# RWKV layers: the units' values repeated by DMA instead of by TensorE, the recurrence in place in SBUF

## The chip, the cores and the metric

The kernel runs on one core of one Trainium2 chip. The metric is the device time of one execution in microseconds. Each engine of the core has its own instruction queue: PE (TensorE, matmuls), DVE (VectorE), ACT (ScalarE), POOL (GpSimd) and SP (SyncE, which here only issues DMAs). ACT issues DMAs too. [...]

## The reference, cut to what matters

Four layers act on x (16 sequences, 100 steps, 512 channels): cross-attention, an RWKV block, cross-attention with a feed-forward part, and an RWKV block again. All is float32. The change is in the RWKV block alone, which runs as layer 1 and layer 3:

```python
w = exp(-exp(time_decay + tanh(xw @ td_w1) @ td_w2))     # b, l, 32 heads, 16
r, k, v = xr @ Wr.T, xk @ Wk.T, xv @ Wv.T                # the same shape
g = silu(xg @ Wg.T)
s = state[:, 2:18].reshape(b, 32, 16, 16)
for t in range(l):                                       # per head, i is the row, j the column
    a = k[t][i] * v[t][j]
    out[t][j] = sum_i r[t][i] * (u[i] * a + s[i, j])
    s = a + w[t][i] * s
x1 = x + (groupnorm(out) * g) @ Wo.T                     # then a channel mix with Wfk, Wfr, Wfv
```

Every state element s[i, j] is a first-order recurrence over 100 steps: it is multiplied by w[i] and k[i] * v[j] is added.

## The kernel before, in words

**Tiling.** The 16 sequences are taken in 4 groups of G = 4; a group has T = 400 columns (4 sequences of 100 steps). The 512 channels are 4 chunks of 128 (8 heads of 16). A pair of group and chunk is numbered C (16 per layer). A chunk has 8 x 16 x 16 = 2048 state elements, so its recurrence is cut in 8 units of 128 partitions x 2 rows x 400 columns. `where(u)` (L1129) gives chunk, column group jg (4 columns) and row pair rp of unit u; a layer has 128 units.

**One unit.** `spread(u)` (L1132) repeats the values v of 4 columns of each head over the partitions with two matmuls against the 0/1 matrix `sel`, shifted by one step, into a PSUM tile of two banks (`vbs`, two in turn); ACT copies the initial state `s0r` into the first step of each sequence. `product(u)` (L1147) multiplies this PSUM tile in place by the k of the row, an SBUF tile, on DVE. `scan(u)` (L1156) runs two tensor_tensor_scan on DVE, from the SBUF tile w and the PSUM tile into an SBUF tile `a`; POOL then multiplies `a` by r in place. `gather(p)` (L1166) sums two units' products over rows with eight matmul instructions into the PSUM bank `acc`, and `norm` (L1178) does the group norm once per chunk.

**Repeated rows.** k, w and r are needed with each row repeated over the partitions. ACT's queue stores them, as they are computed, in DRAM tiles (`store`, L806); `enter(C)` (L1089) loads the plain chunk of v, k and r, and `repeat(C, rp)` (L1099) loads k, w and r of a row pair with four DMAs of 32 partitions each, on SP. v is stored and loaded plain only.

**Order.** A loop over u (L1229 to L1285) writes out the order by hand for PE, DVE, ACT and POOL: wrappers pin the program order (`InOrder`, L69, `mm`, L81). SP's DMAs are not pinned. Each round does spread(u+1), product(u), deferred reads of PSUM banks (`slots.begin`), scan(u), the loads of the next chunk at fixed values of u % 8, gather, and then fills PE with `pieces` for a fixed number of microseconds (`due`, L1276): projections of the next group, output projections of the last one, and, in the last group, the channel mixes. Other PSUM work takes turns in three banks (`slots`, L652); taking a bank forces its outstanding read first.

**Weights** of 1 MB go through a ring of five tiles (`wring`, L42). The channel mix's three are loaded together 35 units before the end (L1247).

Of the kernel before, what the change touches and what calls it, by code (L numbers as in the profile page):

```python
# [35 lines left out]
def xattn_sequence(ctx: ExitStack, tc: tile.TileContext, d: dict, out: bass.AP):  # L36
# [41 lines left out]

    vector, scalar, gpsimd = InOrder(nc.vector), InOrder(nc.scalar), InOrder(nc.gpsimd)

# [555 lines left out]
    def rwkv(n, ws, next_weights, last):  # L636
# [6 lines left out]
        with ExitStack() as es:  # L643
# [5 lines left out]
            psum = es.enter_context(tc.tile_pool(name=f"l{n}a_ps", bufs=1, space=PSUM))  # L649
            vbs = [psum.tile([128, 2, 512], F32, name=f"vb{i}") for i in range(2)]  # L650
            acc = psum.tile([128, 512], F32, name="acc")
            slots = Slots([psum.tile([128, 512], F32, name=f"mm{i}") for i in range(3)])  # L652
            vec = rwkv_vecs(one, n)
# [34 lines left out]

            fold = one.tile([128, 32], F32, name="fold")
            nc.vector.tensor_reduce(fold, ident.rearrange("p (r s) -> p s r", s=32), AX.X, ALU.add)  # L690
            sel = one.tile([128, 16, 32], F32, name="sel")
            for j in range(16):
                nc.vector.tensor_copy(
                    sel[:, j, :].rearrange("p (h i) -> p h i", i=16),
                    fold.rearrange("p (h j) -> p h j", j=16)[:, :, j : j + 1].to_broadcast([128, 2, 16]),
                )


            share = one.tile([128, 2], F32, name="share")
            nc.vector.tensor_reduce(share, heads8.rearrange("p (q h) -> p h q", h=2), AX.X, ALU.add)  # L700
            nc.vector.tensor_scalar(share, share, -1.0 / 16, None, ALU.mult)
            gat = one.tile([128, 4, 32], F32, name="gat")
            nc.gpsimd.memset(gat, 0.0)
            for jg in range(4):
                nc.vector.tensor_copy(
                    gat[:, jg, :].rearrange("p (h g q) -> p g q h", g=4, q=4)[:, jg],
                    heads8.rearrange("p (q h) -> p q h", h=2),
                )
# [6 lines left out]
            s0r = one.tile([128, 4, NC, 4, B], F32, name="s0r")  # L715
            for r in range(4):
                rs = slice(32 * r, 32 * r + 32)
                ps = slots.bank()
                for c in range(NC):
                    for jq in range(4):  # L720
                        mm(
                            out=ps[32 * jq : 32 * jq + 32, c * 64 : (c + 1) * 64], lhsT=ident[rs, rs],
                            rhs=s0[rs, c].rearrange("p b (g q) -> p q g b", q=4)[:, jq],
                            start=True, stop=True,
                        )
                scalar.copy(s0r[:, r].rearrange("p c g b -> p (c g b)"), ps[:, : NC * 64])
# [51 lines left out]
            def chain(us, slot, tag, before, ps, lhs, rhs, read):  # L778
# [18 lines left out]
                piece(us / 2, second, slot, tag)  # L797

            def projections(g, base):
                nm = f"{n}_{g}"  # L800
                to = put[g] = {
                    t: dram.tile([NC, 4, 32, T], F32, tag=t, name=f"d{t}_{nm}")
                    for t in ("k", "v", "r", "w", "g")
                }

                def store(t, c, tile):  # L806
                    nc.scalar.dma_start(out=to[t][c].rearrange("r p t -> (r p) t"), in_=tile)

# [162 lines left out]
            def channels(g, slot):  # L971
# [41 lines left out]
                def keys(co):  # L1013
                    def read(ps):
                        if co == 0:
                            st["kk"] = two.tile([128, NC, T], F32, tag="kk", bufs=1, name=f"kk_{nm}")
# [19 lines left out]
                def values(i):  # L1036
                    b = g * G + i

                    def read(ps):
                        def add():  # L1040
                            th = st[i]
                            vector.scalar_tensor_tensor(th, th, 1.0, ps[:L, :], ALU.add, ALU.mult)
                            vector.scalar_tensor_tensor(xb[b], th, 0.5, xb[b], ALU.mult, ALU.add)
                            if last:
                                nc.sync.dma_start(out=out[b], in_=xb[b])

# [42 lines left out]
            def enter(C):  # L1089
# [4 lines left out]
                for k, bufs in (("v", 2), ("k", 1), ("r", 1)):  # L1094
                    t[k] = two.tile([128, T], F32, tag=f"{k}c", bufs=bufs, name=f"{k}c_{n}_{C}")
                    nc.sync.dma_start(out=t[k], in_=put[g][k][c].rearrange("r p t -> (r p) t"))
                repeat(C, 0)

            def repeat(C, rp):  # L1099
                g, c = C // NC, C % NC  # L1100
                rep = chunks[C]["rep"][rp] = {}
                for t in ("k", "w", "r"):
                    rep[t] = two.tile([128, 2, T], F32, tag=f"{t}rep", bufs=3, name=f"{t}r_{n}_{C}_{rp}")
                    for jq in range(4):
                        nc.sync.dma_start(
                            out=rep[t][32 * jq : 32 * jq + 32],
                            in_=put[g][t][c, 2 * rp : 2 * rp + 2].rearrange("r p t -> p r t"),
                        )

# [21 lines left out]

            def spread(u):  # L1132

                C, jg, rp = where(u)
                p4 = vbs[u % 2][:, :, :T].rearrange("p r (b t) -> p r b t", t=L)
                for i in range(2):
                    rs = slice(64 * rp + 32 * i, 64 * rp + 32 * i + 32)
                    mm(
                        out=p4[:, i, :, 1:L], lhsT=sel[rs, 4 * jg : 4 * jg + 4, :].rearrange("p q m -> p (q m)"),
                        rhs=steps(chunks[C]["v"][rs, :])[:, :, 0 : L - 1], start=True, stop=True,  # L1140
                    )
                g = C // NC
                scalar.copy(
                    p4[:, :, :, 0], s0r[:, 2 * rp : 2 * rp + 2, C % NC, jg, g * G : (g + 1) * G]
                )

            def product(u):  # L1147
                C, jg, rp = where(u)
                p4 = vbs[u % 2][:, :, :T].rearrange("p r (b t) -> p r b t", t=L)
                vector.tensor_tensor(  # L1150
# [5 lines left out]
            def scan(u):  # L1156
                C, jg, rp = where(u)
                rep = chunks[C]["rep"][rp]
                a = products[u] = two.tile([128, 2, T], F32, tag="a", bufs=4, name=f"a_{n}_{u}")
                for i in range(2):  # L1160
                    vector.tensor_tensor_scan(
                        a[:, i, :], rep["w"][:, i, :], vbs[u % 2][:, i, :T], 0.0, ALU.mult, ALU.add
                    )
                gpsimd.tensor_tensor(a, a, rep["r"], ALU.mult)
# [38 lines left out]
            def gates(C):  # L1203
# [3 lines left out]
                chunks[C]["g"] = two.tile([128, T], F32, tag="gc", bufs=5, name=f"gc_{n}_{C}")  # L1207
                nc.sync.dma_start(out=chunks[C]["g"], in_=put[g]["g"][c].rearrange("r p t -> (r p) t"))

# [21 lines left out]
            while u < UNITS + 6 or pieces or slots.due:  # L1231
# [6 lines left out]
                elif u % 32 == 0 and u > 0:  # L1238
# [7 lines left out]
                    output(g - 1, u + 7)  # L1246
                if u == UNITS - 32 - 3:  # L1247
                    cm.update(load(n, "Wfk", "Wfr", "Wfv"))
# [396 lines left out]
    def load(layer, *names):  # L1645
        return {k: load_w(d[f"L{layer}_{k}"], f"l{layer}_{k}") for k in names}

    ws1 = {}
    layer0(lambda: ws1.update(load(1, "Wk", "Wv", "Wr")))
# [72 lines left out]
```

## Time and profile before

| | |
|---|---|
| median of 3 runs | 3527.54 us (3523.34 to 3530.71) |
| profiled execution, its own time | 3530.07 us |
| its span, first to last instruction | 3528.3 us |
| PE busy | 3217.1 us (91%) |
| DVE busy | 1770.8 us (50%) |
| ACT busy | 981.8 us (28%) |
| POOL busy | 1376.4 us (39%) |
| DMA | 216.60 MB, mean 61 GB/s |
| layer 1, first product of the recurrence to the last | about 859 to 1499 us |
| layer 3, the same | about 2785 to 3425 us |

Busy times overlap, since engines run side by side. Shares over the whole span mix four layers with different limits; the two RWKV layers have to be read in their own windows. Almost all pinned instructions carry the line of the wrapper (L77 for DVE, ACT and POOL, L82 for matmuls), so they are told apart by tile names: `vb` is the PSUM tile of a unit, `a` its SBUF tile, `kr`, `wr`, `rr` the repeated rows, `dk`, `dv`, `dr`, `dw`, `dg` the DRAM tiles, `vc`, `kc`, `rc`, `gc` the plain chunks.

### The profile page before, as it was taken

The page shows a single profiled execution, that of the slowest core. Times are in us where ns is not written, and L with a number is a line of the kernel's source. Part 1 is how long each engine was busy: PE and PEld are TensorE (multiplying, and loading weights), DVE is VectorE, ACT ScalarE, POOL GpSimd, SP SyncE. Part 2 cuts the span into 40 slices and gives each one's busy share as a digit, 9 for nine tenths or more (in the row PEclk, how much of TensorE's full clock was granted, in tenths as well). Part 3 has the DMA queues.
Part 4 walks back from the last instruction along what each step waited for, and adds up shares of the span by engine and source line. Part 5 has one row for each costly group of instructions (what it writes and reads, how often), then busy time and mean ns, then how long its engine had stood idle before and what let it go on. Part 6 is the DMA issues. An engine that isn't in the chain of part 4 may idle for free. (4 is left out here: it accounts for less than half of the span.)

```text
span 3528.3 us, 46276 instructions
## 1 busy us (share of the span) xinstructions
PE 3217.1 (91%) x17795; PEld 1432.9 (41%) x17795; DVE 1770.8 (50%) x3570; ACT 981.8 (28%) x1715; POOL 1376.4 (39%) x1036
## 2 busy tenths in 40 slices
PE   6899998868999988988999999789998899998898
PEld 3444443333333333334454555345553333333333
DVE  4777777723777665514333333310001477775651
ACT  1322223222233233321322223211112233333232
POOL 1444444443666665511212111210002466665551
PEclk8999999978999989999999999999997899998998
DMA  5000001012434441101000010110012243433310
GB/s 169 21 31 21 31 21 33 1 56 86 126 108 124 126 146 54 38 27 55 25 19 19 19 31 18 39 53 8 10 57 68 87 129 104 134 115 117 87 29 14
DMA packets 153426, 216.60 MB, mean 61 GB/s; under 512 B 23498, under 2 KB 132106, under 8 KB 153206
## 3 DMA queue, kind: packets, MB, share of 16 engines
q1 hardware_dynamic: 130166, 180.87, 17.3%
q10 hardware_dynamic: 23040, 32.78, 2.6%
q8 instruction: 140, 2.29, 0.3%
q14 instruction: 80, 0.66, 0.1%
HBM read 174.25 MB, written 36.04 MB: 60 GB/s over the span
## 5 line engine op out<-in xcount | busy, mean ns | idle before, releaser
L77 POOL TENSOR_TENSOR a<-a,rr 128x800 f32<-128x800 f32 x256 | 480.9, 1879 | 342.4 <-DVE a L77 269.7
L77 DVE TENSOR_TENSOR_SCAN a<-wr,vb 128x400 f32<-128x400 f32 x512 | 475.7, 971 | 19.8 <-PE acc L82 10.9
L77 DVE TENSOR_TENSOR vb<-vb,kr 128x792 f32<-128x792 f32 x256 | 250.5, 979 | 197.0 <-ACT vb L77 195.5
L77 DVE CUSTOM_DVE_ANT_0 junk<-l_sc,mask 100x361 f32<-100x361 f32 x512 | 273.0, 533 | 90.1 <-PE l_sc L82 73.6
L82 PE MATMUL vb<-vc,sel 32*128 32x396 f32 x1024 | 261.0, 568 | 3.4 <-DVE a L77 2.2
L77 DVE TENSOR_TENSOR pt<-l_sc,maskT 121x400 f32<-121x400 f32 x384 | 193.5, 566 | 89.9 <-PE l_sc L82 89.0
L77 ACT ACTIVATE pt<-pt 121x1600 f32<-121x1600 f32 x96 | 147.6, 1538 | 282.2 <-DVE pt L77 280.7
L1425 DVE CUSTOM_DVE_ANT_0 junk<-l2a_sc,mask 100x361 f32<-100x361 f32 x256 | 136.9, 535 | 172.9 <-PE l2a_sc L82 155.7
L77 POOL TENSOR_TENSOR xj<-tm,ext 128x400 f32<-128x400 f32 x160 | 152.8, 962 | 174.3 <-DVE tm L77 168.0
L77 DVE SCALAR_TENSOR_TENSOR tm<-mm,vec,sx 128x400 f32<-128x400 f32 x160 | 99.9, 631 | 235.6 <-PE mm L82 190.9
L1461 POOL TENSOR_TENSOR pa<-pt,pt 121x1600 f32<-121x1600 f32 x16 | 57.2, 3574 | 366.8 <-ACT pt L1456 366.8
L63 PE MATMUL h<-yTb,l_fc 128*128 128x400 f32 x512 | 175.3, 505 | 8.2 <-ACT yTb L229 8.2
L1642 DVE TENSOR_TENSOR x<-pb,x 100x512 f32<-100x512 f32 x16 | 12.8, 799 | 338.3 <-DMA pb<-po 332.7
L82 PE MATMUL v<-l_v_w,ct 128*121 128x512 f32 x384 | 180.0, 613 | 0.0
L82 PE MATMUL k<-ct,l_k_w 128*128 128x361 f32 x512 | 173.0, 481 | 7.3 <-DVE mv_l2a L207 7.3
L77 POOL TENSOR_TENSOR pa<-pt,pt 121x1600 f32<-121x1600 f32 x32 | 114.7, 3586 | 165.5 <-ACT pt L77 165.5
L63 PE MATMUL p<-l_proj,h 128*128 128x512 f32 x384 | 165.4, 592 | 0.0
L77 ACT COPY vb<-s0r 128x8 f32<-128x8 f32 x256 | 43.0, 168 | 408.7 <-PE vb L82 322.9
L82 PE MATMUL l_sc<-kz,qz 32*100 32x361 f32 x1024 | 117.1, 528 | 42.6 <-DVE pt L77 21.7
L82 PEld LDWEIGHTS vb<-vc,sel 32*128 32x128 f32 x1024 | 84.8, 190 | 146.9 <-issue 107.3
L82 PE MATMUL mm<-l_Wo,gc 128*100 128x512 f32 x256 | 124.6, 629 | 8.4 <-POOL gc L77 8.4
L63 PEld LDWEIGHTS h<-yTb,l_fc 128*128 128x128 f32 x512 | 98.1, 192 | 83.3 <-ACT yTb L229 10.1
(258 smaller groups left out, 5305.6 us busy)
## 6 DMA issues: line engine op xcount, KB each, us to landing
kr<-dk SPq DMA_DIRECT2D x256, 100.0 KB
wr<-dw SPq DMA_DIRECT2D x256, 100.0 KB
rr<-dr SPq DMA_DIRECT2D x256, 100.0 KB
ct<-in_ctxT SPq DMA_DIRECT2D x32, 722.0 KB
dk<-k ACTq DMA_DIRECT2D x32, 200.0 KB
kc<-dk SPq DMA_DIRECT2D x32, 200.0 KB
dw<-wd ACTq DMA_DIRECT2D x32, 200.0 KB
dv<-v ACTq DMA_DIRECT2D x32, 200.0 KB
```

What stands on the lines that cost most here:

```text
L63: nc.tensor.matmul(out=ps, lhsT=lhs(c), rhs=rhs(c), start=(c == 0), stop=(c == n - 1))
L77: return lambda *args, **kw: tc.keep_in_program_order(op(*args, **kw))
L82: pin(nc.tensor.matmul(**kw))
L1425: nc.vector.tensor_tensor_reduce(out=junk, in0=ss[r][:L, :S2], in1=t["mask"], scale=-1.0, scalar=FLT_MAX, op0=ALU.add, op1=ALU.min, accum_ ...
L1461: nc.gpsimd.tensor_tensor(t["pa"], t["pt"][0], pt, ALU.add)
L1642: nc.vector.tensor_tensor(x, pb[:, i, :], x, ALU.add)
```

## The change

The repetition of v leaves PE. v is stored in DRAM like k, w and r, one element later, so that a read which begins one element before a row is the row shifted by one step. `fetch(u)` reads it with two DMAs of 64 partitions straight into the SBUF tile `a` of the unit, which now has 6 buffers instead of 4, two rounds ahead. ACT's copy of the initial state (`first`) writes into `a` one round ahead. The product, the scans and POOL's multiplication all work in place in `a`.

The partitions of a unit are ordered head, row, column, where before they were ordered column, head, row; the DRAM layout of k, v, r, w puts the four row residues of a partition quartet next to each other, so a row pair is one run of 800 elements, and `repeat` needs one DMA of 128 partitions where it needed four. Stores and plain loads are now four DMAs of 32 partitions instead of one of 128. The loads of a chunk's repeated rows are spread over more rounds, and SP's DMAs in the loop are pinned in program order. The PSUM banks of `vbs` go to `slots`, which has 7 banks instead of 3. `gat` and the set-up of `s0r` follow the new order; `sel` is gone. The squared keys of the channel mix share a ring with its inputs. The channel mix's weights come in quarters, from 46, 40 and 35 units before the end.

```diff
-            vbs = [psum.tile([128, 2, 512], F32, name=f"vb{i}") for i in range(2)]
             acc = psum.tile([128, 512], F32, name="acc")
-            slots = Slots([psum.tile([128, 512], F32, name=f"mm{i}") for i in range(3)])
+            slots = Slots([psum.tile([128, 512], F32, name=f"mm{i}") for i in range(7)])
...
+            def rows_of(g, t, c):
+                if t == "g":
+                    return [(slice(0, 128), put[g][t][c].rearrange("r p t -> (r p) t"))]
+                rows = put[g][t][1:] if t == "v" else put[g][t]
+                rows = rows[c * 128 * T : (c + 1) * 128 * T].rearrange("(p r t) -> r p t", r=4, t=T)
+                return [(slice(32 * r, 32 * r + 32), rows[r]) for r in range(4)]
...
                 def store(t, c, tile):
-                    nc.scalar.dma_start(out=to[t][c].rearrange("r p t -> (r p) t"), in_=tile)
+                    for ps, rows in rows_of(g, t, c):
+                        nc.scalar.dma_start(out=rows, in_=tile[ps])
...
-            def repeat(C, rp):
+            def repeat(C, rp, names):
                 g, c = C // NC, C % NC
-                rep = chunks[C]["rep"][rp] = {}
-                for t in ("k", "w", "r"):
+                rep = chunks[C]["rep"].setdefault(rp, {})
+                for t in names:
                     rep[t] = two.tile([128, 2, T], F32, tag=f"{t}rep", bufs=3, name=f"{t}r_{n}_{C}_{rp}")
-                    for jq in range(4):
-                        nc.sync.dma_start(
-                            out=rep[t][32 * jq : 32 * jq + 32],
-                            in_=put[g][t][c, 2 * rp : 2 * rp + 2].rearrange("r p t -> p r t"),
-                        )
+                    x = put[g][t]
+                    n0 = x.offset + (c * 128 + 2 * rp) * T
+                    sync.dma_start(
+                        out=rep[t], in_=bass.AP(x.tensor, n0, [[4 * T, 32], [0, 4], [1, 2 * T]])
+                    )
...
-            def spread(u):
+            def fetch(u):
                 C, jg, rp = where(u)
-                p4 = vbs[u % 2][:, :, :T].rearrange("p r (b t) -> p r b t", t=L)
-                for i in range(2):
-                    rs = slice(64 * rp + 32 * i, 64 * rp + 32 * i + 32)
-                    mm(
-                        out=p4[:, i, :, 1:L], lhsT=sel[rs, 4 * jg : 4 * jg + 4, :].rearrange("p q m -> p (q m)"),
-                        rhs=steps(chunks[C]["v"][rs, :])[:, :, 0 : L - 1], start=True, stop=True,
-                    )
+                g, c = C // NC, C % NC
+                a = products[u] = two.tile([128, 2, T], F32, tag="a", bufs=6, name=f"a_{n}_{u}")
+                v = put[g]["v"]
+                for h in range(2):
+                    n0 = v.offset + (c * 128 + 64 * h + 16 * jg + 2 * rp) * T
+                    sync.dma_start(
+                        out=a[64 * h : 64 * h + 64],
+                        in_=bass.AP(v.tensor, n0, [[0, 16], [4 * T, 4], [1, 2 * T]]),
+                    )
+
+            def first(u):
+                C, jg, rp = where(u)
                 g = C // NC
                 scalar.copy(
-                    p4[:, :, :, 0], s0r[:, 2 * rp : 2 * rp + 2, C % NC, jg, g * G : (g + 1) * G]
+                    products[u].rearrange("p r (b t) -> p r b t", t=L)[:, :, :, 0],
+                    s0r[:, 2 * rp : 2 * rp + 2, C % NC, jg, g * G : (g + 1) * G],
                 )
...
             def product(u):
                 C, jg, rp = where(u)
-                p4 = vbs[u % 2][:, :, :T].rearrange("p r (b t) -> p r b t", t=L)
+                p4 = products[u].rearrange("p r (b t) -> p r b t", t=L)
                 vector.tensor_tensor(
                     p4[:, :, :, 1:L], p4[:, :, :, 1:L],
                     chunks[C]["rep"][rp]["k"].rearrange("p r (b t) -> p r b t", t=L)[:, :, :, 0 : L - 1],
...
-                a = products[u] = two.tile([128, 2, T], F32, tag="a", bufs=4, name=f"a_{n}_{u}")
+                a = products[u]
                 for i in range(2):
-                    vector.tensor_tensor_scan(
-                        a[:, i, :], rep["w"][:, i, :], vbs[u % 2][:, i, :T], 0.0, ALU.mult, ALU.add
-                    )
+                    vector.tensor_tensor_scan(a[:, i, :], rep["w"][:, i, :], a[:, i, :], 0.0, ALU.mult, ALU.add)
                 gpsimd.tensor_tensor(a, a, rep["r"], ALU.mult)
...
                 unit = 0 <= u < UNITS
+                if 0 <= u + 2 < UNITS:
+                    fetch(u + 2)
                 if 0 <= u + 1 < UNITS:
-                    spread(u + 1)
+                    first(u + 1)
                 if unit:
                     product(u)
...
                     if at == 4:
                         enter(C)
+                    elif at == 5:
+                        repeat(C, 0, "w")
                     elif at == 6:
-                        repeat(C, 1)
+                        repeat(C, 0, "r")
                         bonus(C, 0)
                     elif at == 7:
+                        repeat(C, 1, "kw")
                         bonus(C, 1)
                 C = u // 8
+                if 0 <= C < NC * NG and at == 0:
+                    repeat(C, 1, "r")
```

More of the change, by code (lines that the diff above doesn't have):

```diff
@@ L77, in __getattr__ @@
             return lambda *args, **kw: tc.keep_in_program_order(op(*args, **kw))
-    vector, scalar, gpsimd = InOrder(nc.vector), InOrder(nc.scalar), InOrder(nc.gpsimd)
+    vector, scalar, gpsimd, sync = map(InOrder, (nc.vector, nc.scalar, nc.gpsimd, nc.sync))
     def mm(**kw):
@@ L687, in rwkv @@
             nc.vector.tensor_tensor(center, ident, mean, ALU.subtract)
[L689 to L695, printed above, removed]
-                )
+            hq = one.tile([128, 2, 4], F32, name="hq")
+            nc.vector.tensor_reduce(hq, ident.rearrange("p (h i q) -> p h q i", h=2, q=4), AX.X, ALU.add)
             share = one.tile([128, 2], F32, name="share")
-            nc.vector.tensor_reduce(share, heads8.rearrange("p (q h) -> p h q", h=2), AX.X, ALU.add)
+            nc.vector.tensor_reduce(share, hq, AX.X, ALU.add)
             nc.vector.tensor_scalar(share, share, -1.0 / 16, None, ALU.mult)
@@ L705, in rwkv @@
                 nc.vector.tensor_copy(
-                    gat[:, jg, :].rearrange("p (h g q) -> p g q h", g=4, q=4)[:, jg],
-                    heads8.rearrange("p (q h) -> p q h", h=2),
+                    gat[:, jg, :].rearrange("p (h g q) -> p g h q", g=4, q=4)[:, jg], hq
                 )
@@ L715, in rwkv @@
             s0r = one.tile([128, 4, NC, 4, B], F32, name="s0r")
+            pair = one.tile([128, 32], F32, name="pair")
+            nc.vector.tensor_reduce(pair, ident.rearrange("p (r s) -> p s r", s=32), AX.X, ALU.add)
+            fold = two.tile([128, 4, 128], F32, tag="stage", bufs=6, name="fold")
+            nc.gpsimd.memset(fold, 0.0)
+            for q in range(4):
+                nc.vector.tensor_copy(fold[:, q, :].rearrange("p (s q) -> p q s", q=4)[:, q], pair)
             for r in range(4):
@@ L719, in rwkv @@
                 for c in range(NC):
-                    for jq in range(4):
+                    for q in range(4):
                         mm(
-                            out=ps[32 * jq : 32 * jq + 32, c * 64 : (c + 1) * 64], lhsT=ident[rs, rs],
-                            rhs=s0[rs, c].rearrange("p b (g q) -> p q g b", q=4)[:, jq],
-                            start=True, stop=True,
+                            out=ps[:, c * 64 : (c + 1) * 64], lhsT=fold[rs, q, :],
+                            rhs=s0[rs, c].rearrange("p b (g q) -> p q g b", q=4)[:, q],
+                            start=(q == 0), stop=(q == 3),
                         )
@@ L801, in projections @@
                 to = put[g] = {
-                    t: dram.tile([NC, 4, 32, T], F32, tag=t, name=f"d{t}_{nm}")
-                    for t in ("k", "v", "r", "w", "g")
-                }
+                    t: dram.tile([NC * 128 * T + (t == "v")], F32, tag=t, name=f"d{t}_{nm}") for t in "kvrw"
+                }
+                to["g"] = dram.tile([NC, 4, 32, T], F32, tag="g", name=f"dg_{nm}")
+                sync.dma_start(out=to["v"][0:1].rearrange("(p t) -> p t", t=1), in_=eps[0:1, :])
                 def store(t, c, tile):
-                    nc.scalar.dma_start(out=to[t][c].rearrange("r p t -> (r p) t"), in_=tile)
+                    for ps, rows in rows_of(g, t, c):
+                        nc.scalar.dma_start(out=rows, in_=tile[ps])
                 rows = [xb[g * G + i] for i in range(G)]
@@ L1015, in read @@
                         if co == 0:
-                            st["kk"] = two.tile([128, NC, T], F32, tag="kk", bufs=1, name=f"kk_{nm}")
+                            st["kk"] = two.tile([128, NC, T], F32, tag="xm", bufs=3, name=f"kk_{nm}")
                         rl = two.tile([128, T], F32, tag="tm", bufs=4, name=f"rl_{nm}_{co}")
@@ L1044, in add @@
                             if last:
-                                nc.sync.dma_start(out=out[b], in_=xb[b])
+                                sync.dma_start(out=out[b], in_=xb[b])
                         slots.read_later(ps, add)
@@ L1095, in enter @@
                     t[k] = two.tile([128, T], F32, tag=f"{k}c", bufs=bufs, name=f"{k}c_{n}_{C}")
-                    nc.sync.dma_start(out=t[k], in_=put[g][k][c].rearrange("r p t -> (r p) t"))
-                repeat(C, 0)
-            def repeat(C, rp):
+                    for ps, rows in rows_of(g, k, c):
+                        sync.dma_start(out=t[k][ps], in_=rows)
+                repeat(C, 0, "k")
+            def repeat(C, rp, names):
                 g, c = C // NC, C % NC
-                rep = chunks[C]["rep"][rp] = {}
-                for t in ("k", "w", "r"):
+                rep = chunks[C]["rep"].setdefault(rp, {})
+                for t in names:
                     rep[t] = two.tile([128, 2, T], F32, tag=f"{t}rep", bufs=3, name=f"{t}r_{n}_{C}_{rp}")
-                    for jq in range(4):
-                        nc.sync.dma_start(
-                            out=rep[t][32 * jq : 32 * jq + 32],
-                            in_=put[g][t][c, 2 * rp : 2 * rp + 2].rearrange("r p t -> p r t"),
-                        )
+                    x = put[g][t]
[3 more added lines that the diff above has]
+                    )
             def bonus(C, part):
@@ L1207, in gates @@
                 chunks[C]["g"] = two.tile([128, T], F32, tag="gc", bufs=5, name=f"gc_{n}_{C}")
-                nc.sync.dma_start(out=chunks[C]["g"], in_=put[g]["g"][c].rearrange("r p t -> (r p) t"))
+                sync.dma_start(out=chunks[C]["g"], in_=rows_of(g, "g", c)[0][1])
             def output(g, slot):
@@ L1246, in rwkv @@
                     output(g - 1, u + 7)
-                if u == UNITS - 32 - 3:
-                    cm.update(load(n, "Wfk", "Wfr", "Wfv"))
+                for k, at_u in (("Wfk", UNITS - 46), ("Wfr", UNITS - 40), ("Wfv", UNITS - 35)):
+                    if 0 <= u - at_u < NC:
+                        load_part(cm, n, k, u - at_u)
                 if u >= UNITS and not nws and not any(p[3] == ("wo", NG - 1) for p in pieces):
@@ L1646, in load, with load_part @@
         return {k: load_w(d[f"L{layer}_{k}"], f"l{layer}_{k}") for k in names}
+    def load_part(ws, layer, k, c):
+        if c == 0:
+            ws[k] = wring.tile([128, NC, 512], F32, tag="w", name=f"l{layer}_{k}")
+        sync.dma_start(out=ws[k][:, c, :], in_=d[f"L{layer}_{k}"][c * 128 : (c + 1) * 128, :])
     ws1 = {}
```

## The prediction

> **What bounds the kernel now.** I read the windows first, over the stretch of layer 1 in which groups 0 to 2 run their recurrence (860 to 1295 us) and its last group (1295 to 1486.5), then the same two of layer 3. The columns after the window's length are the busy us of PE, weight load, DVE, ACT and POOL, then the granted PE clock, the DMA share and GB/s.
>
> ```profile
> 860.00:1295.00 435.00, 417.80 (x1586) 158.08 (x1584) 319.96 (x396) 137.85 (x292) 288.45 (x231) 0.94 0.40 119
> 1295.00:1486.50 191.50, 169.98 (x573) 62.53 (x574) 109.60 (x136) 70.27 (x133) 106.66 (x93) 0.88 0.22 62
> 2775.00:3215.00 440.00, 421.87 (x1599) 161.39 (x1600) 316.96 (x392) 143.49 (x300) 290.90 (x238) 0.93 0.39 118
> 3215.00:3420.00 205.00, 180.45 (x613) 66.84 (x613) 116.97 (x146) 75.50 (x145) 112.59 (x96) 0.89 0.23 64
> ```
>
> PE is busy 418 of 435 us, DVE 320, POOL 288: PE is the bound, and DVE plus POOL together (608) exceed the window, so these two overlap today. The same windows restricted to the tile vb show 285 DVE instructions, three per unit (one product, two scans), so 95 units in the first stretch and, from 283, 94 in that of layer 3: 435/95 = 4.58 and 440/94 = 4.67 us per unit. The costliest groups give the pieces of a unit:
>
> ```profile
> L77 POOL TENSOR_TENSOR a<-a,rr 128x800 f32<-128x800 f32 x256 | 480.9, 1879 | 342.4 <-DVE a L77 269.7
> L77 DVE TENSOR_TENSOR_SCAN a<-wr,vb 128x400 f32<-128x400 f32 x512 | 475.7, 971 | 19.8 <-PE acc L82 10.9
> L77 DVE TENSOR_TENSOR vb<-vb,kr 128x792 f32<-128x792 f32 x256 | 250.5, 979 | 197.0 <-ACT vb L77 195.5
> L82 PE MATMUL vb<-vc,sel 32*128 32x396 f32 x1024 | 261.0, 568 | 3.4 <-DVE a L77 2.2
> ```
>
> The product and scans read one operand from PSUM (vb) and one from SBUF (kr, wr). After the change both operands are in SBUF. So I looked for DVE instructions that already have two SBUF operands. In the answer for tile x (min/median/max ns):
>
> ```profile
> L77 DVE TENSOR_TENSOR x<-mm,x x32: 691/692/694, 1044.0 to 3465.5; 100x512 f32<-100x512 f32 x32
> L77 DVE SCALAR_TENSOR_TENSOR x<-th_1b,x x16: 691/692/1650, 1341.4 to 1598.0; 100x512 f32<-100x512 f32 x16
> L1642 DVE TENSOR_TENSOR x<-pb,x x16: 691/693/1751, 2369.1 to 2668.5; 100x512 f32<-100x512 f32 x16
> ```
>
> With PSUM and SBUF (mm, x) none of 32 exceeds 694 ns; with two SBUF operands some take 1650 or 1751. The timeline around the 1650, DVE first and then POOL (start us, us):
>
> ```profile
> 1471.01 1.65 DVE L77 SCALAR_TENSOR_TENSOR x<-th_1b,x 100x512 f32<-100x512 f32 x1
> ```
> ```profile
> 1470.23 1.88 POOL L77 TENSOR_TENSOR a<-a,rr 128x800 f32<-128x800 f32 x1
> 1472.07 2.12 POOL L77 TENSOR_TENSOR sx_1b<-ext_1b 128x400 f32<-128x400 f32 x2
> ```
>
> POOL's product ends at 1472.11; the DVE instruction ends at 1472.66, 0.55 us later, where 0.69 is its own length. It stood still until POOL was done. The POOL pair then takes 2.12, not 2 x 0.854 = 1.71. Each side blocks the other, and a hand-over saves about 0.14 us (0.69 - 0.55).
>
> [...] The trace has 979 with a PSUM operand, and 692 against 693 at 512 elements for PSUM and SBUF, so I take no gain from leaving PSUM. [...]
>
> **The change part by part.**
> Removed: the spread matmuls. The tile's windows give PE 96.45 us in the first stretch, but some run beside matmuls of mm in other row groups (at 1074.12 both start together). Taking the union of PE's intervals without them leaves 354 of 418 us and 357 of 422 in the two long stretches, 144.5 of 170 and 152.6 of 180 in the last groups. So 64, 65, 25 and 28 us of PE work go. In the long stretches PE alone would allow (435 - 64)/95 = 3.9 us per unit.
>
> Moved to SBUF: per unit one product of 0.98 and two scans of 0.97, 2.92 us on DVE[...]. POOL's work reads SBUF, too, apart from 12 memsets of 0.1: 288.45/95 = 3.04 us per unit (the product 1.88, xj 0.60, the rest og, gc, rk, xm, sx). No two-SBUF scan is in the trace; bounds are that it holds the path for its 0.97 or not at all. I take the first, as it reads two SBUF streams like the product. Then DVE and POOL exclude each other: 2.92 + 3.04 = 5.96 us per unit. POOL has 209 instructions of size over 95 units, 2.2 per unit; each can be one hand-over to it and one back, so up to 4.4 x 0.14 = 0.62 is saved: 5.34 at best. Neither side runs while a result crosses (the scan pair that ends at 1087.66 releases the POOL product at 1087.88: 0.2 us), where the other has nothing ready. I take 5.34 + 0.16 = 5.5. DVE's other work, 51 us or 0.53 per unit, has a PSUM operand or one input; it can lie under POOL's time.
> Long stretches: 95 x (5.5 - 4.58) = +87, 94 x (5.5 - 4.67) = +78, together **+165 us**.
> Last groups: two-operand DVE 84.2 plus POOL 106.7 is 191, less 78 POOL instructions x 2 x 0.14 = 22: 169 to 191, in a window of 191.5; PE would need 144.5 plus its present idle 21.5. Between -22 and 0 each if only one bounds; the two chains wait on each other there, so I take 0.
>
> Added: the fetch, two transfers of 200 KB per unit, 95 x 0.41 = 39 MB on 52 MB now (119 GB/s x 435 us). Today's rate at full share is 119/0.40 = 297 GB/s, so 91 MB need 306 of 522 us. Hidden. One pair takes 0.41 MB/297 = 1.4 us[...]. It starts when gather has freed the product of unit u-4, in iteration u-1, and is wanted by the ACT copy in iteration u+1: at least one period, 5.5 us, covers it. That copy is a new wait: ACT's stores, tanh, exp and bank reads queue behind it, and PE waits for these. On SP, now in program order, the fetch stands behind chunk loads that wait for stores of k, v, r; issues cost 0.42 us each, some 35 per chunk against 28, 15 us of a chunk's 44: hidden. Taken at 0; if the cover goes, see the second rival.
> ACT: 12 more stores per chunk at 0.33 us, 4 us of 44 on an engine that is a third busy: 0. Seven banks in place of three: PE idles only 17 us in the stretch, and PE is no longer the bound: 0, at best -17 per layer. The sixteen set-up copies (173 ns each, 3 us) lie under the wait for the layer's loads: 0. Weight loads in quarters: 0.
>
> **Sum:** profiled execution 3530.07 (span 3528.3 and 1.8 around it) + 165 = 3695; the median shown, 3527.54, is 2.5 lower, so **3693**.
>
> **Rivals.**
> First, it is faster. [...] DVE's hold is 0.98 per unit; 0.98 + 3.04 = 4.0, or 3.7 with hand-overs, and PE bounds at 3.9: -65 and -65, and half of the last groups' 53: -26. That is -156, 3372; with some blocking of products, about 3400. The point of decision is a hold of 4.62 + 0.62 - 3.04 = 2.2 us per unit. For it: no two-SBUF scan is in the trace. Against it: all lengthened instructions are of the two-operand kind.
> Second, still slower. The fetch lands late: sixteen reads of the same rows at once, or SP held up. From 5.5 us after its gather on, ACT's copy stops DVE. At 1 us per unit it adds 189: 3880. For it: no such repeated read is in the trace. Against it: the DMA share of 0.58.
> Third, a small loss or none: hand-overs all saved (5.34: 72 + 63 = +135), last groups -44, banks worth -17 per layer: +57, 3584, or lower.
>
> **How the numbers follow.** The lock with the fetch hidden 0.70, with 3600 to 3850 as its own range (5.34 and -44 below; 5.96 + 0.2 per unit, 150 + 140 = +290 and 30 of new waits above); late fetch 0.10; faster 0.16; small loss or none 0.04. The range 3540 to 3880 holds the first, half of the second and the last, 0.79. A difference of 0.2% (7 us) is about what can be told: faster 0.16, same 0.03, slower 0.81.
>
> **What would show it.** Product and scan means rising from 0.98 and 0.97 towards 1.5 or more, and POOL's a from 1.88 to over 2.2, both by blocking; PE falling to about 75% in the long stretches; a unit of 5.5 us; DMA waits still small. I am wrong if scans keep 0.97 beside a running POOL product, or if the copy of the first state waits for DMA.

## The result and the profile after

The changed kernel takes 3736.14 us (3732.84 to 3737.62, 4 runs) against 3526.94 us, a ratio of 1.0592 (95% interval 1.0573 to 1.061). The profiled execution took 3736.31, its span is 3734.3. The forecast was 3693, range 3540 to 3880, so the loss is 209 us where 165 was forecast.

The costliest groups on DVE and POOL (busy us, mean ns, then the idle time in front and its releaser):

```profile
L77 DVE TENSOR_TENSOR_SCAN a<-wr,a 128x400 f32<-128x400 f32 x512 | 801.2, 1604 | 40.4 <-ACT a L77 33.8
L77 POOL TENSOR_TENSOR a<-a,rr 128x800 f32<-128x800 f32 x256 | 593.2, 2318 | 301.3 <-DVE a L77 97.4
L77 DVE TENSOR_TENSOR a<-a,kr 128x792 f32<-128x792 f32 x256 | 306.2, 1196 | 4.4 <-DMA a<-dv 4.4
L77 POOL TENSOR_TENSOR xj<-tm,ext 128x400 f32<-128x400 f32 x160 | 228.4, 1435 | 138.0 <-DVE tm L77 137.9
```

The last of them before the change:

```profile
L77 POOL TENSOR_TENSOR xj<-tm,ext 128x400 f32<-128x400 f32 x160 | 152.8, 962 | 174.3 <-DVE tm L77 168.0 <-DMA kr<-dk 4.7 <-DMA rr<-dr 1.1
```

The same instructions on the same shapes: the scan went from 971 to 1604 ns, the product from 979 to 1196, POOL's product from 1879 to 2318, its xj from 962 to 1435. Little idle time is left in front of the DVE instructions (4 us before the product, which had 197, and 40 before the scans, which had 20), so DVE looks like a busy engine. The distribution in the answer for tile a (min/median/max ns) shows that a good part of this is standing, which counts as busy: the scan's median is 1680 ns, its shortest 957.

```profile
L77 DVE TENSOR_TENSOR_SCAN a<-wr,a x512: 957/1680/2714, 894.6 to 3637.7; 128x400 f32<-128x400 f32 x171
L77 DVE TENSOR_TENSOR a<-a,kr x256: 949/952/2585, 875.9 to 3632.1; 128x792 f32<-128x792 f32 x128
L77 POOL TENSOR_TENSOR a<-a,rr x256: 1862/2386/2625, 897.2 to 3639.0; 128x800 f32<-128x800 f32 x128
```

The same three before the change, from the answers for tiles vb and a:

```profile
L77 DVE TENSOR_TENSOR_SCAN a<-wr,vb x512: 954/969/989, 867.3 to 3430.1; 128x400 f32<-128x400 f32 x171
L77 DVE TENSOR_TENSOR vb<-vb,kr x256: 958/980/992, 859.4 to 3424.5; 128x792 f32<-128x792 f32 x128
L77 POOL TENSOR_TENSOR a<-a,rr x256: 1861/1878/1901, 869.2 to 3431.3; 128x800 f32<-128x800 f32 x128
```

The shortest of each kind is nearly as before, 957, 949 and 1862 ns; the maxima, and the medians of scan and POOL, are not. The timeline of one unit, DVE first and then POOL, shows who waits for whom:

```profile
897.09 0.95 DVE L77 TENSOR_TENSOR a<-a,kr 128x792 f32<-128x792 f32 x1
898.13 3.39 DVE L77 TENSOR_TENSOR_SCAN a<-wr,a 128x400 f32<-128x400 f32 x2
```
```profile
897.24 2.54 POOL L77 TENSOR_TENSOR a<-a,rr 128x800 f32<-128x800 f32 x1 [0.93 <-DVE a L77]
```

The next unit's product starts at 897.09, before POOL is released; POOL's multiplication of the last unit, issued at 897.24, stands until the product ends at 898.04 and then runs its 1.74 us, to 899.78; the first scan, issued at 898.13, stands until then. The pair of scans takes 3.39 us where it took 1.85.

This is no single case. Of the 192 scans of groups 0 to 2 in layer 1, 147 began while a POOL instruction ran, and 138 of these took over 1.05 us; of the other 45 none took over 1.0 us. Before the change, 127 of these 192 began beside POOL, and none took over 1.0 us. So DVE instructions with two SBUF operands and POOL's work hold each other up: above, POOL stands for the product (2.54 us, 1.88 before) and the scans for POOL (3.39, 1.85 before). That is what "holds the path" means in the forecast; what in the chip makes one stand for the other was not shown.

In the long stretches the windows read (busy us of PE, weight load, DVE, ACT, POOL; granted PE clock, DMA share, GB/s):

```profile
876.00:1417.00 541.00, 393.57 (x1234) 153.54 (x1235) 475.44 (x406) 148.16 (x309) 410.27 (x247) 0.81 0.57 170
2899.00:3438.00 539.00, 386.50 (x1231) 148.81 (x1232) 478.66 (x405) 147.63 (x308) 410.40 (x246) 0.82 0.57 169
```

PE is down from 96% to 73%, DVE up from 74% to 88%, POOL from 66% to 76%. To find where the 206 us of span went, I cut both traces at the same instructions: the first set-up instruction of a layer, its first normed row, its first scan, its 193rd scan (unit 96, where the last group begins) and its last. The part from the first scan to the 193rd is called the long stretch.

| us | before | after | difference |
|---|---|---|---|
| start to set-up of layer 1 | 741.5 | 747.5 | +6.0 |
| layer 1: set-up to first normed row | 11.5 | 33.9 | **+22.4** |
| to the first scan | 114.2 | 113.2 | -1.0 |
| first scan to the 193rd | 448.9 | 532.6 | **+83.7** |
| to the end of the last scan | 189.8 | 187.9 | -1.9 |
| to set-up of layer 3 | 1158.2 | 1152.4 | -5.8 |
| layer 3: set-up to first normed row | 13.9 | 36.3 | **+22.3** |
| to the first scan | 114.5 | 114.3 | -0.2 |
| first scan to the 193rd | 448.9 | 530.5 | **+81.6** |
| to the end of the last scan | 189.7 | 190.2 | +0.5 |
| to the end | 97.2 | 95.6 | -1.6 |

The long stretches lose 165.3 us and the set-ups 44.7; the rest sums to -4.

The set-up is the rearranged initial state, `s0r`. The timeline of PE there, before and after:

```profile
749.76 2.85 PE L82 MATMUL mm<-s,ident 32*32 32x64 f32 x128 [14.23 <-DMA s<-in_s]
```
```profile
755.78 25.19 PE L82 MATMUL mm<-s,fold 32*128 32x64 f32 x128 [14.30 <-DMA s<-in_s]
```

As many instructions, 128, and as many columns; but 32 rows onto 32 columns before (`32*32`) and onto 128 after (`32*128`). At 288 ns each (the median in the answer for tile s) the old ones ran some 13 at a time (128 x 0.288 / 2.85); at 402 ns the new ones ran two at a time. The weight loads that go with them take 328 ns in the median, where they took 146, and fill the same 25 us. Whether the loads or the matmuls hold the pace is not shown.

### The profile page after: what moved, and what is told of

It is laid out like the page before. It is cut to its first block, busy times and chain, and to the rows that moved or that the text cites. A ratio compares the mean times of both kernels' runs of the same rounds, so it can differ in the third digit from the quotient of the medians.

```text
span 3734.3 us, 45535 instructions
## 1 busy us (share of the span) xinstructions
PE 3117.2 (83%) x16771; PEld 1433.6 (38%) x16771; DVE 2138.3 (57%) x3548; ACT 977.5 (26%) x1715; POOL 1662.5 (45%) x1038
## 5 line engine op out<-in xcount | busy, mean ns | idle before, releaser
L77 DVE TENSOR_TENSOR_SCAN a<-wr,a 128x400 f32<-128x400 f32 x512 | 801.2, 1604 | 40.4 <-ACT a L77 33.8
L77 POOL TENSOR_TENSOR a<-a,rr 128x800 f32<-128x800 f32 x256 | 593.2, 2318 | 301.3 <-DVE a L77 97.4
L77 DVE TENSOR_TENSOR a<-a,kr 128x792 f32<-128x792 f32 x256 | 306.2, 1196 | 4.4 <-DMA a<-dv 4.4
L77 POOL TENSOR_TENSOR xj<-tm,ext 128x400 f32<-128x400 f32 x160 | 228.4, 1435 | 138.0 <-DVE tm L77 137.9
L82 PE MATMUL mm<-rk,ones 128*128 128x400 f32 x64 | 52.9, 930 | 218.0 <-POOL rk L77 130.6
L82 PE MATMUL acc<-a,gat 128*32 128x400 f32 x1024 | 157.4, 603 | 29.4 <-POOL a L77 29.2
L77 ACT COPY a<-s0r 128x8 f32<-128x8 f32 x256 | 50.5, 201 | 450.2 <-DMA a<-dv 239.0
L77 POOL TENSOR_TENSOR pa<-pa,pt 119x1600 f32<-119x1600 f32 x32 | 114.5, 3578 | 42.5 <-ACT pt L77 42.3
```

The source lines that it names most:

```text
L77: return lambda *args, **kw: tc.keep_in_program_order(op(*args, **kw))
L82: pin(nc.tensor.matmul(**kw))
```

## The experiments

Each run was timed next to the kernel before on the same chip (3527.5, 3527.4 and 3527.9 us in the three sets). e1 to e4 are of the first set, e5, e7 and e8 of the second, e9 to e11 of the third.

### e1: the set-up of the initial state

```diff
+            banks = [slots.bank() for r in range(4)]
+            for q in range(4):
+                for r in range(4):
+                    rs = slice(32 * r, 32 * r + 32)
+                    mm(
+                        out=banks[r][:, : NC * 64], lhsT=fold[rs, q, :],
+                        rhs=s0[rs].rearrange("p c b (g q) -> p q c g b", q=4)[:, q],
...
             for r in range(4):
-                rs = slice(32 * r, 32 * r + 32)
-                ps = slots.bank()
-                for c in range(NC):
-                    for q in range(4):
-                        mm(
-                            out=ps[:, c * 64 : (c + 1) * 64], lhsT=fold[rs, q, :],
-                            rhs=s0[rs, c].rearrange("p b (g q) -> p q g b", q=4)[:, q],
...
```

> The change with its set-up of the initial state in 16 matmuls of 256 columns in place of 64 of 64 columns, the four row residues taking turns so that neighbours use different row groups. If the set-up is a cost of its own, the stretch from the layer's first set-up instruction to the first normed row falls from 34-36 us back to some 12-15 us in each layer, and the time from 3736 to about 3691. If it lies under a later wait (the first scan comes only when the next group's projections have begun), less than half of it shows: 3715 or more. The two long stretches keep their +82 us against before either way.

Measured: 3688.31 us, ratio 1.0463 (1.0447 to 1.0479). The PE timeline of the set-up:

```profile
749.61 3.82 PE L82 MATMUL mm<-s,fold 32*128 32x256 f32 x32 [14.38 <-DMA s<-in_s]
```

25.19 us became 3.82; set-up to first normed row is 13.4 and 16.0 us, for 12 to 15 expected. So 20.5 and 20.3 of the 22.4 and 22.3 us came back, and the time fell by 48 (3736 - 3688): the set-up was on the path. The edit changes the number of the matmuls, their columns and their order at once; which of these did it is open. The long stretches stay at 531.0 and 530.8 us. e1 is the base of the next runs.

### e2: scans from SBUF, values still by PE

From the kernel before, with one sharing of buffers taken from the change to make room:

```diff
             def spread(u):
...
+                a = products[u] = two.tile([128, 2, T], F32, tag="a", bufs=5, name=f"a_{n}_{u}")
...
-                    p4[:, :, :, 0], s0r[:, 2 * rp : 2 * rp + 2, C % NC, jg, g * G : (g + 1) * G]
+                    a.rearrange("p r (b t) -> p r b t", t=L)[:, :, :, 0], s0r[:, 2 * rp : 2 * rp + 2, C % NC, jg, g * G : (g + 1) * G]
...
-                    p4[:, :, :, 1:L], p4[:, :, :, 1:L],
+                    products[u].rearrange("p r (b t) -> p r b t", t=L)[:, :, :, 1:L], p4[:, :, :, 1:L],
...
-                        a[:, i, :], rep["w"][:, i, :], vbs[u % 2][:, i, :T], 0.0, ALU.mult, ALU.add
+                        a[:, i, :], rep["w"][:, i, :], a[:, i, :], 0.0, ALU.mult, ALU.add
...
-                            st["kk"] = two.tile([128, NC, T], F32, tag="kk", bufs=1, name=f"kk_{nm}")
+                            st["kk"] = two.tile([128, NC, T], F32, tag="xm", bufs=3, name=f"kk_{nm}")
```

> The kernel before, with the values still repeated by PE into PSUM and the product still reading PSUM, but writing SBUF, so that only the scans have two SBUF operands. Theory [...]: the scan's mean rises from 0.97 to 1.4 us or more, POOL's product from 1.88 to over 2.1, and DVE hold 1.94 + POOL 3.04 = 4.98 per unit, less hand-overs, comes near PE's 4.58: 0.2 to 0.5 us per unit, 3570 to 3630. Rival [...]: scan 0.97, POOL 1.88, time within 10 us of 3527.

Measured: 3646.89 us, ratio 1.0343 (1.0325 to 1.0362); long stretches 499.7 and 499.9 us, +51 each. The answer for tile a:

```profile
L77 DVE TENSOR_TENSOR_SCAN a<-wr,a x512: 957/1408/3127, 868.8 to 3547.4; 128x400 f32<-128x400 f32 x171
L77 DVE TENSOR_TENSOR a<-vb,kr x256: 948/952/984, 860.8 to 3541.5; 128x792 f32<-128x792 f32 x128
L77 POOL TENSOR_TENSOR a<-a,rr x256: 1862/1879/3153, 871.5 to 3548.5; 128x800 f32<-128x800 f32 x128
```

This run has no DMA repetition, no pinned SP queue and no new partition order, and still the scans stand. The product, which here reads one operand from PSUM, never exceeds 984 ns. So a scan with two SBUF operands is held up beside POOL (mean 1387 ns, 971 before), the one assumption for which the forecast had no line. The expected rise of POOL's product did not come (median 1879): in 67 of the 96 units of the first long stretch it begins while the product runs, which does not hold it up here, and then the scans wait for it. The time is 17 us above the expected interval; the last groups, which the expectation did not count, are 10 us longer each.

### e3 and e5: without POOL's multiplication

The same edit to e1 (e3) and to the kernel before (e5):

```diff
-                gpsimd.tensor_tensor(a, a, rep["r"], ALU.mult)
+                if C % NC == 3 and C // NC == NG - 1:
+                    gpsimd.tensor_tensor(a, a, rep["r"], ALU.mult)
```

> e1 without POOL's multiplication by r in all chunks but the last of the last group: that part of the recurrence's output is left out, so the time is that of a kernel which does less. Theory: POOL's reads fall from 3.04 to 1.16 us per unit, DVE hold plus POOL to 2.92 + 1.16 = 4.1 less hand-overs; PE allows 3.9; unit 4.0 to 4.4 us, time 3430 to 3520. Rival (fetches or queues bound the unit[...]): little change from e1, 3650 or more.

> Control for e3: the kernel before without POOL's multiplication by r in all chunks but the last of the last group (that part of the output is left out). Theory: PE bounds and POOL runs beside DVE, so nothing is gained by taking 1.88 us per unit from POOL: 3500 to 3530. Rival (POOL's multiplication is on the chain of every unit whatever the operands): 3430 or less.

Measured: e3 3503.99 us, ratio 0.9939 (0.9924 to 0.9954), long stretches 458.1 and 452.9. e5 3508.79 us, ratio 0.9943 (0.9927 to 0.9959), long stretches 449.3 and 449.3, against 448.9 of before. The same instruction costs 3688 - 3504 = 184 us with both DVE operands in SBUF, and 3527 - 3509 = 19 us, none of it in the long stretches, with one of them in PSUM. This control is weaker than it looks, for PE is busy 418 of 438 us in e5's stretch, so that little could be gained there whatever POOL did:

```profile
867.00:1305.00 438.00, 417.65 (x1575) 159.07 (x1574) 319.81 (x398) 142.66 (x299) 115.47 (x142) 0.92 0.41 122
```

And e3 stays at 4.77 us per unit (458.1/96), above the 4.0 to 4.4 that was expected. Some standing is left in it (scans 1202 ns in the mean, beside POOL's other work), but e4, which has none, is no faster per unit (459.1/96 = 4.78 us): beneath the standing lies a second limit.

### e4: values by DMA, operands in PSUM

From e1; the fetch goes to a tile of its own, and ACT copies it to PSUM:

```diff
-            slots = Slots([psum.tile([128, 512], F32, name=f"mm{i}") for i in range(7)])
+            vbs = [psum.tile([128, 2, 512], F32, name=f"vb{i}") for i in range(2)]
+            slots = Slots([psum.tile([128, 512], F32, name=f"mm{i}") for i in range(3)])
...
-                a = products[u] = two.tile([128, 2, T], F32, tag="a", bufs=6, name=f"a_{n}_{u}")
+                a = raws[u] = two.tile([128, 2, T], F32, tag="vr", bufs=2, name=f"vr_{n}_{u}")
...
+                scalar.copy(
+                    p4[:, :, :, 1:L], raws.pop(u).rearrange("p r (b t) -> p r b t", t=L)[:, :, :, 1:L]
+                )
```

and product and scan read `vbs` as before the change.

> The values still repeated by DMA, in the new partition order and with the SP order of the change and the shorter set-up of e1, but ACT copies them from SBUF to two PSUM tiles, so product and scans read one PSUM and one SBUF operand again; three banks for the other work, as before. Theory [...]: product 0.98, scan 0.97, POOL 1.88, PE now free of the spread matmuls: 4.0 to 4.3 us per unit in the long stretches, time 3420 to 3480, faster than both. Rival (the DMA repetition itself, late fetches or the pinned SP queue, costs the time): 3600 or more with POOL and DVE at their short durations and idle.

Measured: 3517.48 us, ratio 0.9972 (0.9962 to 0.9982). Against e1 that is -171 us, with 210 us of ACT work more. Scan 970, product 981, POOL's product 1878 ns: no standing at all, although 128 of the 192 scans of the first long stretch began beside POOL. The edit changes more than the place of an operand: three banks instead of seven, and a fetch whose buffer is freed by ACT's copy and not by the gather. But it keeps the DMA repetition, and the standing is what went. The long stretches are still 459.1 and 458.1 us, 10 and 9 more than before, and the gain is in the last groups (-20 and -14); the profiled execution took 3525.61 us, 8 above the median. The expected 3420 to 3480 was missed. The window and the copy's group:

```profile
878.00:1337.00 459.00, 372.63 (x1224) 145.67 (x1221) 322.77 (x404) 218.49 (x399) 298.25 (x244) 0.85 0.69 204
```
```profile
L77 ACT COPY vb<-vr 128x792 f32<-128x792 f32 x256 | 210.3, 821 | 369.2 <-DMA vr<-dv 144.7 <-DVE a L77 73.9 <-DMA dw<-wd 25.9
```

No engine is full (PE 81%). The copy waits 145 us for the fetch in the whole run, and in this stretch DVE waits 102 us for ACT's copies.

### e8: e3 without the loads of r

```diff
                 for t in names:
+                    if t == "r" and C < NC * NG - 1:
+                        continue
```

> e3 (no multiplication by r, which is left out of the output) also without the loads of the repeated r that only this multiplication reads: 0.8 of some 7.6 MB per chunk less. If what holds e3 at 4.77 us per unit is the DMA load, the long stretches shrink by up to a tenth, 458 to 415-440 us, time 3430 to 3490. If it is PE, ACT or the order of the queues, e3's 3504 stays within 10 us.

Measured: 3487.61 us, ratio 0.9894 (0.9876 to 0.9911), long stretches 450.9 and 446.2. The time is inside what the DMA load was to give, but the stretches are only 7 us shorter each for a tenth of the bytes, not 18 to 43. The sheer bytes are a part of the second limit at most.

### e7: half of the values by DMA, half by PE

From e4; odd units are spread by PE with a `sel` in the new partition order:

```diff
             def fetch(u):
                 C, jg, rp = where(u)
+                if rp:
+                    return
...
+                if rp:
+                    for i in range(2):
+                        rs = slice(64 * rp + 32 * i, 64 * rp + 32 * i + 32)
+                        mm(
+                            out=p4[:, i, :, 1:L], lhsT=sel[rs, jg, :],
+                            rhs=steps(chunks[C]["v"][rs, :])[:, :, 0 : L - 1], start=True, stop=True,
+                        )
+                else:
...
```

> As e4, but only every other unit's values come by DMA and an ACT copy into PSUM; the others are spread by PE as before, in the new partition order. If e4's 4.77 us per unit come from the DMA load (share 0.69 in its stretch, waits of ACT for the fetch) and the ACT copies, halving both lets the unit go to 4.2 to 4.5: 3430 to 3490. If they come from something that e4 shares with this kernel whole (stores in four pieces, the pinned SP queue, the chunk's bonus), it stays within 15 us of e4's 3517.

Measured: 3490.9 us, ratio 0.9897 (0.988 to 0.9914); long stretches 455.0 and 434.4 us, last groups 177.8 and 176.6. That is just past the upper edge of what was expected; only the second long stretch, at 4.53 us per unit, is clearly shorter than in e4.

### e9, e10, e11: the bonus matmul two rounds later

`bonus` adds the term with u to the output, in three parts: POOL makes the product rk, a matmul sums it and DVE multiplies the sum by v, further matmuls add the result to `acc`. In e4 PE stands 108 us at the first matmul, which waits for POOL's rk, in e7 53, in e1 141, in the kernel before 17. The edit moves this part from round 7 to round 1 of the next chunk; the last part stays in round 2.

```diff
                     elif at == 7:
                         repeat(C, 1, "kw")
-                        bonus(C, 1)
...
+                if 0 <= C < NC * NG and at == 1:
+                    bonus(C, 1)
```

> e4 with the chunk's bonus matmul, which waits for POOL's rk, issued two rounds later on PE (round 1 of the chunk in place of round 7 of the one before). In e4 PE stands 108 us in all at that matmul. If this wait at the head of PE's queue is what holds e4 at 4.77 us per unit, the long stretches fall by some 40 us each, time 3430 to 3460. If the fetches hold it, PE's wait only moves to another instruction: 3500 or more.

> e7 with the same move; there PE stands 53 us at the bonus matmul. If that wait is on the path: 3440 to 3465. Otherwise within 10 us of 3491.

> e1 (the change with the short set-up) with the same move; there PE stands 141 us at the bonus matmul. [...] PE's wait is slack and the time stays within 15 us of e1's 3688. If PE's wait is on the path of the change itself, it falls by 60 to 140 us, to 3550-3630.

Measured: e9 (from e4) 3498.14 us, ratio 0.9917 (0.9898 to 0.9936), long stretches 467.8 and 470.5, longer than in e4, and last groups 151.5 and 164.3; its profiled execution took 3507.29 us, 9 above the median. e10 (from e7) 3462.58 us, ratio 0.9816 (0.9802 to 0.9831), long stretches 441.5 and 435.4. e11 (from e1) 3680.75 us, ratio 1.0433 (1.0415 to 1.045), long stretches 532.5 and 529.7 against e1's 531.0 and 530.8.

e11 stays within the 15 us that were expected if PE's wait is slack. But the move took little of the wait away: the matmuls of the last part now wait 106 us for DVE's rk, by the answer for tile rk (us, times):

```profile
  DVE rk L77: 106.0, 22
```

PE's idle time in the two long stretches fell only from 148.4 and 145.9 us (e1) to 135.4 and 131.7. That these 13 and 14 us shortened neither stretch agrees with a pace set by the standing of DVE and POOL; it is no proof of it. In e9, PE is no less idle in the long stretches (92.5 and 94.1 us, in e4 86.4 and 84.5), so e9 does not test what it was made for, and its time lies between the two outcomes that were named. e10's time is inside what was expected if the wait is on the path, but PE's idle time in its long stretches, 49.1 and 47.0 us, is that of e7, 49.0 and 45.8, so this is not shown either. ACT's idle time before the copy, released by the fetch, is 172 us in e9 and 11 in e10, from the answers for tile vr of the two:

```profile
  DMA vr<-dv: 172.2, 62
```
```profile
  DMA vr<-dv: 10.6, 4
```

e10's long stretches are 26 and 35 us shorter than those of e9. So late fetches are a likely part of the second limit, but e10 halves the copies with them, and the two are not told apart. Whether a fetch is late for the queue, the buffers or the DMA engines was not separated.

e10 is the fastest: about 65 us under the kernel before. Its windows in the two long stretches:

```profile
868.00:1290.00 422.00, 383.82 (x1384) 147.40 (x1382) 314.42 (x392) 170.97 (x335) 282.93 (x225) 0.92 0.58 171
2760.00:3195.00 435.00, 387.96 (x1413) 149.66 (x1411) 321.30 (x404) 181.76 (x352) 297.85 (x243) 0.91 0.57 171
```

## Why the prediction was right, and where it was not

**The long stretches.** The sum had +165 us at 5.5 us per unit; measured +165.3 at 5.55 and 5.53 (532.6/96, 530.5/96). That the totals agree to a microsecond is luck: 5.34 to 5.96 was possible, and the forecast counted 95 and 94 units at 4.58 and 4.67 us, where the long stretches have 96 at 4.68 (448.9/96), for which its 5.5 gives +158. The cause is shown: e2 makes +51 of some +83 us per layer appear without the DMAs, by the scans alone; e4 makes the standing vanish with the DMAs kept; and in the change it is the scans beside POOL that are drawn out (138 of 147 over 1.05 us). Since e4 without standing is still 10 and 9 us above before, some 73 us per layer are the standing's, an estimate from these two; the rest would stay without it.

**The scan's hold.** The step with no line in the profile ("I take the first, as it reads two SBUF streams like the product") was right: 0.97 to 1.39 us in e2. The first rival, in which scans are not held up, falls with it.

**An argument that was misread.** That "all lengthened instructions are of the two-operand kind" does not hold. Of the 17 DVE instructions of before that took over a quarter longer than the median of their kind, all of them beside POOL, seven are a tensor_scalar that reads one large tensor, x, and two values per row, all from SBUF:

```profile
L1339 DVE TENSOR_SCALAR xn_l2a<-x,mv_l2a,rstd_l2a x16: 538/546/1518, 1603.7 to 1897.5; 100x512 f32<-100x512 f32 x16
```

So the line that the forecast had against its first rival was weaker than it said; only e2 decided it. That DVE's other work with one input can lie under POOL's time was the forecast's estimate, and these seven (up to 1518 and 1500 ns, with medians of 546 and 544) speak against it.

**Last groups taken at 0:** -1.9 and +0.5.

**The step that failed** is the set-up. The forecast priced the sixteen copies that were removed (they built `sel`) at 0, and had no term for the matmuls of the initial state, which the change made anew: +22.4 and +22.3. e1 gave 20.5 and 20.3 back. With this term the sum is 3693 + 45 = 3738, where 3736 was measured. The diff showed it (an output slice of 32 partitions became one of 128), and the forecast didn't follow it.

**"Hidden" for the fetch** was right for the time and wrong as a reading of slack. "DMA waits still small" failed, and one of the signs named for being wrong came: the copy of the first state waits for DMA, 239 us in the changed kernel. DVE idles only 4.4 us before products and 40 before scans, so this didn't cost much there; but e3 shows 4.77 us per unit directly beneath, not PE's 3.9. The second rival, late fetches, had its mechanism present, under cover of the standing. That one period covers a pair was an estimate from the bytes and the rate of before (1.4 us); a pair's time from issue to landing was not measured.

**Signs.** POOL's product over 2.2 (2.32) and PE at about 75% (73%) came as said. The product was to rise "towards 1.5 or more" and has 1.20: in 75 of 95 cases of the first long stretch it is already running when POOL's multiplication begins, and the scans take the waiting (1.60). A product that stands for nobody takes 0.95 us (median 952 ns, 980 before), where the forecast took 0.98; in e2, which still reads one operand from PSUM but writes SBUF, the median is 952, too.

**PE's relief** was smaller than the union of intervals said: 394 us busy in the stretch, where 354 over 95 units was expected. The granted clock is 0.81 there, 0.94 before. It mattered little, as PE was idle for 147 of the 541 us.

## What to carry to other kernels

Before an operand of a DVE instruction is moved from PSUM to SBUF, see whether the other operand is in SBUF and whether POOL works at the same time: if so, look whether DVE's and POOL's times in that stretch add up. Here they nearly did: 2.92 + 3.04 = 5.96 us per unit, 5.34 with all hand-overs saved, and 5.55 and 5.53 were measured. The evidence was in the max of min/median/max of instructions that already had two SBUF operands (1650 and 1751 ns, median 692 and 693); a tensor_scalar from SBUF was drawn out, too (1518, median 546). Then ask what lies under this limit: here it was not PE (81% busy in e4), and without the standing the long stretches would still have been 10 us longer than before. Price every line that a diff adds to a set-up like one in the loop; here the missing term was that of matmuls whose output grew from 32 to 128 partitions (2.85 to 25.19 us).

## What the runs showed that was not expected

In the set-up, matmuls with 32 rows onto 32 columns ran many at a time: 128 of them, 288 ns each, in 2.85 us. The same count onto 128 columns took 25.19, and 32 of them with four times the columns, with neighbours in different row groups, 3.82.

In the first long stretch, the granted PE clock was lower where PE was less busy: 0.94 at 96% before, 0.92 at 91% in e10, 0.85 at 81% in e4, 0.81 at 73% in the change. It does not hold everywhere: in layer 1's last group it was 0.94 at 87% in e4 and 0.88 at 89% before. No run here tests why.
